# Where a planned instruction stream puts its counts, feature loads and pair steps

## The chip, the cores and the metric

One core of a Trainium2 chip runs the whole program. The metric is the device time of one execution in microseconds (us). The engines are TensorE (PE in the profile; PEld is its weight load), VectorE (DVE), ScalarE (ACT), GpSimd (POOL) and SyncE (SP, which here only issues DMAs). GpSimd issues DMAs too, from the same queue in which it computes.

## The reference

Four layers on one graph of 2708 nodes with 512 features; each adds its result to x and normalizes. Cut to what is computed:

```python
deg = maximum((adj != 0).sum(-1), 1)
# layer 0: weight a entry > 0 by itself plus 1/sqrt(number of such entries in its row)
inc = adj + mask / sqrt(sum(mask)) ;  x = layernorm(x + (inc @ x) / inc.sum(-1))
# layer 1: attention over the entries that are not 0, and a second branch
s = x @ W_sa @ a_l + (x @ W_sa @ a_r).T
e = where(adj != 0, exp(-leaky_relu(s)), 0)
x_a = (e / (e.sum(1) + 1e-5)) @ (x @ W_sa) ;  x_b = adj @ (x @ W_gcn) + b_gcn
x = layernorm(x + sigmoid(gate_a * x_a + gate_b * x_b))
# layer 2: powers of the adjacency
p = x ; o = x @ W[0] ;  for i in 1..3: p = adj @ p ; o += p @ W[i]
x = layernorm(x + o)
# layer 3: normalized adjacency with deg
x = layernorm(x + relu((d^-1/2 (adj + I) d^-1/2 @ x + x) @ W_out + b_out))
```

## The kernel before

All matrices are float32. Rows and columns are cut into two halves of 1354 nodes (h = 0 low, 1 high), and an adjacency product is done by a seven-product scheme for 2x2 blocks: products P1 to P7 of sums of the adjacency blocks (11, 12, 21, 22; the sums s1 to s4 are made in place by VectorE at line 419) with sums of the feature blocks (B11, B12, B21, B22; the sums T1 to T4, in lines 226 to 238). B12 is kept in the tile of T3. k counts tiles of 128 nodes, ten in each half and a rest.

There are seven sweeps over the adjacency. S[0] is layer 0; S[1] multiplies the plain adjacency (branch b of layer 1, and it writes the sums s1 to s4 to memory for later); S[2] multiplies the attention weights; S[3] to S[5] are the hops of layer 2; S[6] is layer 3. The first three go through four ranges of columns (384, 384, 256, 330 wide; S[0] begins with the 256), the others through two groups.

The order of the work is written by hand: `at(position, function)` puts a piece of work into a list, sorted by position. Sweep s starts at position 28 s, and a range takes 7 positions, one for each product; one position ("unit") of a 384-wide range is 40 matmul instructions on TensorE, of a 256- or 330-wide range likewise. So S[2] + 21.62 is in the fourth range of the third sweep. The framework then plans the instructions: each engine's queue is filled by list order among those that its own estimates hold ready, so an instruction may come earlier or later than in the list. Two things restrict this: all instructions of the first 3 times `strict` are tied to the one before them on their engine, and so are those of pieces put in with `hold` (True, or one engine). Such a tie (`add_manual_dep`, NoSync) only fixes the order in a queue [...]

Names and lines that the change and the prediction's steps touch:

- `next_x` (line 256): feature loads of S[1] from X1, which layer 0 writes range by range, issued on GpSimd (line 150 inside `move`); `x_sums` and `x_last` make T1 to T4.
- `layernorm` (line 598): bn_stats on VectorE, then the inverse root by a power on GpSimd (line 605), then VectorE or ScalarE scale (607, 610, 614).
- `extra1` (line 1031): `tally` counts the nonzero entries of each column of the first to fourth range in S[1] for `deg`: 44 VectorE instructions a range (lines 1039, 1042) into a mask tile, then `end` (six one-column matmuls, line 1056) and `rows`.
- `prep2` (line 1158): in S[2] the attention weights, two ScalarE instructions (1163, 1164) and one on VectorE (1165) for each tile.
- `pairs2` (line 1199): for two tiles of nodes at a time, one of each half, after a range of S[2]: b(0), b(1) multiply by W_sa (`seven`, line 692, accumulated by 701), c is the sigmoid, d and e the residual and layernorm, f the transposes (642), z the node sums (1193), g(0), g(1) the product with hop weights. There are 3 + 3 + 2 such pairs; the last range has no pairs.
- `sums2` (line 1139): sums of the weights for the pairs, partly in the memory of the mask tiles.
- `ext_loads`, `ext_sums` (lines 1331, 1340): added tiles; the hops multiply by [adjacency; transposed X2], and the sums of the X2 blocks are made here and stored (tensor Es, line 1345).
- `done6` (line 1639): end of layer 3 for one group and half.
- "ring" is a pool of 38 tiles for adjacency tiles, sums, ScalarE's e and the added tiles; an instruction that takes one waits until its last reader is done.

Of the kernel before, what the change touches and what calls it, by code (L numbers as in the profile page):

```python
# [28 lines left out]
KT = 11  # L29
# [17 lines left out]
KW = 2 * K2  # L47
# [21 lines left out]
def gnn_kernel(ctx: ExitStack, tc: tile.TileContext, x, adjT, w_sa, a_sa, w_gcn, b_gcn, wab, bab, w_hop, w_out,  # L69
# [106 lines left out]
    events = []  # L176

    held = set()

    def at(pos, fn, hold=False):  # L180

        def go():
            n = len(nc.cur_bb.bb.instructions)
            fn()
            for i in range(n, len(nc.cur_bb.bb.instructions)):
                if hold is True or nc.cur_bb.bb.instructions[i].engine == hold.engine:
                    held.add(i)

        events.append((pos, len(events), go if hold else fn))
# [60 lines left out]
    def x_load(src, k, s, eng):  # L250
        w = wt(k)
        q = x_source(src, k)[("B11", "B12", "B21", "B22").index(s)]
        t = b12_tile(k) if s == "B12" else new_x(s, k)
        move(eng, t[:w], q)

    def next_x(base, src, sums=0.95, halves=-0.25):


        q = nc.gpsimd

        ql = nc.scalar if base == S[1] else q
        at(base + 1.3, lambda: rest_x(src, ql))
        for k in range(KW):
            f = k / KT
            if (k * P) < RANGES[-1][0]:
                at(base - 5.8 + f, lambda k=k: x_load(src, k, "B11", q))
                at(base - 1.85 + f, lambda k=k: x_load(src, k, "B22", q))
                at(base - 1.84 + f, lambda k=k: x_load(src, k, "B12", q))
                at(base + (0.03 if base == S[1] else -1.15) + f, lambda k=k: x_sums(k), True)
                at(base - 0.85 + f, lambda k=k: x_load(src, k, "B21", q))  # L270
                at(base + 1.5 + f, lambda k=k: x_last(k), True)
            else:
                at(base + halves + 0.05 * (k - 8), lambda k=k: x_load(src, k, "B22", ql))
                at(base + max(halves, 0.1) + 0.05 * (k - 8), lambda k=k: x_load(src, k, "B21", ql))
                at(base + sums + 0.03 * (k - 8), lambda k=k: x_sums(k), True)
                at(base + 2.6 + 0.03 * (k - 8), lambda k=k: x_last(k), True)
# [321 lines left out]
    def layernorm(dsts, y, w, on_scalar=False, late=None):  # L598
        st = small.tile([P, 6], F32, name="st")
        nc.vector.bn_stats(st[:w], y[:w])  # L600
        mv = small.tile([P, 2], F32, name="mv")
        nc.vector.bn_aggr(mv[:w], st[:w])
        rstd = small.tile([P, 2], F32, name="rstd")
        nc.vector.tensor_scalar(rstd[:w, 0:1], mv[:w, 1:2], EPS, None, ALU.add)  # L604
        nc.gpsimd.tensor_tensor(rstd[:w, 1:2], rstd[:w, 0:1], neg_half[:w], ALU.pow)  # L605
        if on_scalar:
            nc.vector.scalar_tensor_tensor(rstd[:w, 0:1], mv[:w, 0:1], -1.0, rstd[:w, 1:2], ALU.mult, ALU.mult)
        for d, c0, c1 in dsts:
            if on_scalar:
                fn = lambda d=d, c0=c0, c1=c1: nc.scalar.activation(d[:w], y[:w, c0:c1], AF.Identity,  # L610
                                                                    bias=rstd[:w, 0:1], scale=rstd[:w, 1:2])
                fn() if late is None else late.append(fn)
                continue
            nc.vector.tensor_scalar(d[:w], y[:w, c0:c1], mv[:w, 0:1], rstd[:w, 1:2], ALU.subtract, ALU.mult)
# [125 lines left out]
    def tiles_of(R0, n):  # L740
        return list(range(R0 // P, (R0 + n + P - 1) // P))
# [287 lines left out]
    at(S[1] + 2.33 + 0.95 * (i - 1), scores_over)  # L1029

    def extra1(pb, r, R0, n, A):
        ts = tiles_of(R0, n)

        def tally(h, key, w=P):

            a = A[(r,) + key]
            if (R0, h) not in deg:
                deg[R0, h] = d = mask_tile()
                nc.vector.tensor_scalar(d[:w, :n], a[:w, :n], 0.0, None, ALU.not_equal)
            else:  # L1040
                d = deg[R0, h]
                nc.vector.scalar_tensor_tensor(d[:w, :n], a[:w, :n], 0.0, d[:w, :n], ALU.not_equal, ALU.add)  # L1042

        for ij, p in (("11", -0.6), ("21", 0.05), ("22", 1.05), ("12", 3.6)):
            for k in range(KW):
                at(pb + p + 0.8 * k / KT, lambda ij=ij, k=k: tally(int(ij[0]) - 1, (ij, k)), r == 0)
        for h, p in ((1, 2.0), (0, 4.5)):
            at(pb + p, lambda h=h: tally(h, ("r", h), KA))
            at(pb + p, lambda h=h: tally(h, ("r32", h), 32))

        def end(h):
            d = deg.pop((R0, h))
            ps = bank("ds", [P, 4])
            for i, q in enumerate(ts):
                wq = wt(q)
                nc.tensor.matmul(ps[:wq, i : i + 1], d[:, q * P - R0 : q * P - R0 + wq], ones_bf[:, 0:1], start=True,
                                 stop=True)
            for i, q in enumerate(ts):
                wq = wt(q)
                o = rdeg[:wq, h * KT + q : h * KT + q + 1]  # L1060
                nc.vector.tensor_scalar(o, ps[:wq, i : i + 1], 1.0, None, ALU.max)
                nc.vector.tensor_scalar(diag[:wq, h, q : q + 1], o, 1.0, None, ALU.add)
                nc.vector.reciprocal(o, o)

        def rows(h):
            to_rows(rdeg[:, h * KT + ts[0] : h * KT + ts[-1] + 1], len(ts),
                    DROW[h][0, ts[0] * P : (ts[-1] + 1) * P].rearrange("(k i) -> k i", i=P))

        at(pb + 2.6, lambda: end(1))
        at(pb + 3.7, lambda: rows(1))  # L1070
        at(pb + 5.2, lambda: end(0))
        at(pb + 6.3, lambda: rows(0))
# [78 lines left out]
            o, w = (W[2][2 * c + 1], w_sa) if k == 2 else (W[3][c][:, HD:], w_hop[3])  # L1151
            nc.scalar.dma_start(out=o, in_=w[c * P : (c + 1) * P, HD:])

    at(S[2] + 6.4, sums2)
    at(S[2] + 23.4, lambda: again(2))
    at(S[2] + 24.2, lambda: again(3))

# [9 lines left out]
    def extra2(pb, r, R0, n, A):  # L1167
        def rows(h):
            row[R0, h] = tmp("row")
            m = (n + P - 1) // P  # L1170
            src = SROW[R0, h][0:1, :]
            nc.sync.dma_start(out=row[R0, h][:, : m * P].rearrange("p (k i) -> p k i", i=P),
                              in_=bass.AP(tensor=src.tensor, offset=src.offset, ap=[[0, P], [P, m], [1, P]]))

        def share(o, s, t, w):
            nc.vector.tensor_scalar(o, s, 1e-5, None, ALU.add)
            nc.vector.reciprocal(o, o)
            nc.vector.tensor_tensor(o, o, gate[:w, t, 0:1], ALU.mult)

        at(pb - 1.6, lambda: rows(0))  # L1180
        at(pb - 1.0, lambda: rows(1))
        at(pb + 5.2, lambda: run_sums(R0, n, 0, share))
        at(pb + 4.7, lambda: run_sums(R0, n, 1, share))
# [15 lines left out]
    def pairs2(p0, R0, n, C, tiles):  # L1199
        Y = {}  # L1200
        at(p0 + 0.2, lambda: Y.update(row_sums({(i, c): C[1 - i, c] for i in range(2) for c in range(DC)}, n)))
        for i, (t0, lo, w) in enumerate(tiles):
# [6 lines left out]
            def b(part, ts=ts, lo=lo, w=w, xb=xb, H=H):  # L1209
                seven(part, Y, W[9], H, lo, w, xb, [rd[t][:w] for t in ts], xb)  # L1210
# [35 lines left out]
            at(p - 0.25, a)  # L1246
            at(p + 0.15, d)
            for j in range(2):
                at(p + 0.26 * j, lambda j=j, b=b: b(j))
                at(p + 0.45 + 0.02 * j, lambda j=j, e=e: e(j))  # L1250
                at(p + 0.84 + 0.06 * j, lambda j=j, f=f: f(j), nc.tensor)
                at(p + 1.22 + 0.22 * j, lambda j=j, g=g: g(j), nc.tensor)
            at(p + 0.4, c)
            at(p + 0.92, z)

    def done2(p0, dp, last, R0, n, h, C, tiles):
        if not last:
# [288 lines left out]


    for i in range(4):
        for g, p in enumerate((S[2] + 19.3 + 1.1 * i, S[3] + 6.6 + 1.3 * i)):
            a = ({}, g, i // 2, i % 2)  # L1550
            at(p, lambda a=a: ext_loads(*a))
            at(p + 0.5 + 0.6 * g, lambda a=a: ext_sums(*a))
# [53 lines left out]
        for r in (64, 96):  # L1606
            nc.gpsimd.dma_start(out=diag_r[r : r + 32, 2:3], in_=d2[KA - KR : KR, KT - 1 :])

    at(S[2] + 4.0, diag_ends)

    def finish_degrees():
        t = small.tile([24, P], F32, name="fd", bufs=1)
# [26 lines left out]
    def done6(p0, dp, g, i0, n, h, cc, tiles):  # L1639

        end = (g, h) == (1, 0)
        def finish(s, lo, w, x, y):

            nc.vector.scalar_tensor_tensor(x[:w], y[:w], 0.0, x[:w], ALU.max, ALU.add)
            layernorm([(x, 0, D)], x, w, True)
            r0 = i0 + s * n + lo
            move(nc.sync, out[h * NH + r0 : h * NH + r0 + w, :], x[:w])
# [77 lines left out]
    for n, i in enumerate(list(nc.cur_bb.bb.instructions)):  # L1725
        p = last if n < 3 * strict else done if n in held else {}
        if i.engine in p:
            tc.add_manual_dep(i, p[i.engine].name,
                              mybir.DependencyInfo(mybir.DependencyClass.NoSync, mybir.DependencyReason.DATA),
                              reason="order of the list")  # L1730
        if n < strict:
            last[i.engine] = i
        done[i.engine] = i


# [35 lines left out]
```

## Time and profile before

| | us |
|---|---|
| median of 3 runs | 2844.96 (2844.59 to 2845.8) |
| the profiled execution, its own time | 2845.44 |
| its span, first to last instruction | 2843.7 |
| TensorE busy | 2802.4 |
| VectorE busy | 2247.7 |
| GpSimd busy (DMA issue counted) | 617.2 |
| ScalarE busy | 533.7 |

Landmarks by the first matmul of product P1 in the timeline: fourth range of S[0] at 324.98, S[1] at 415.86, S[2] at 834.71, its second range at 945.39, third at 1084.96, fourth at 1193.69. The page gives busy shares and the costliest groups of instructions; the windows view gives busy time of each engine in stretches (length, PE, PEld, DVE, ACT, POOL, each with a count, then the granted TensorE clock, the DMA share and GB/s); the waits view has who waited for whom: us in total, times, longest; the timeline has start, length, engine, line, operation, out<-in, and in brackets the engine's idle time before it and what ended it. A float32 matmul appears as two matmul instructions.

### The profile page before, as it was taken

The numbers are of one execution on the slowest core, as the hardware profiler recorded it, in microseconds if no ns is written. First come the engines' busy times: TensorE is split into PE (matmuls) and PEld (weight loads), VectorE is DVE, ScalarE is ACT, GpSimd is POOL, SyncE is SP. The second block draws the span as 40 slices with busy tenths as digits, with TensorE's granted clock in tenths as the row PEclk, the third lists the DMA queues.
The fourth block names the chain that finished last, engine by engine and source line by source line (L and its number), as shares of the span: only waits on it lengthen the run. The fifth ranks groups of instructions, "written<-read, shape, count | busy, mean of one in ns | idle before, by whom it ended". The sixth has DMA issues, their size and how long they took to land.

```text
span 2843.7 us, 38764 instructions
## 1 busy us (share of the span) xinstructions
PE 2802.4 (99%) x11550; PEld 1939.7 (68%) x11550; DVE 2247.7 (79%) x5862; ACT 533.7 (19%) x1124; POOL 617.2 (22%) x1114
## 2 busy tenths in 40 slices
PE   7999999999999999999999999999999999999998
PEld 6899765658755667866666666666666666666665
DVE  6999699668737676775699778897888878899987
ACT  4644100101155353450100000000000100100001
POOL 0223223214310011223113033030330211601202
PEclk9999999999999999999999999999999999999999
DMA  8765476446534242665678667566675666854542
GB/s 234 241 195 184 140 228 218 150 131 196 189 92 139 78 152 69 203 194 158 205 205 255 192 208 234 163 210 203 197 235 173 189 194 180 243 167 146 179 142 90
DMA packets 370291, 511.72 MB, mean 180 GB/s; under 512 B 63632, under 2 KB 323460, under 8 KB 370080
## 3 DMA queue, kind: packets, MB, share of 16 engines
q1 hardware_dynamic: 303544, 371.61, 44.1%
q0 software_dynamic: 49376, 126.39, 13.3%
q10 hardware_dynamic: 17160, 11.24, 1.4%
q8 instruction: 92, 1.51, 0.2%
q14 instruction: 119, 0.97, 0.1%
HBM read 425.35 MB, written 83.66 MB: 179 GB/s over the span
## 4 chain that ended last, share of the span: by engine, by line
PE 86%; DVE 7%; issue 2%; DMA 1%; SPq 1%; ACT 1%; POOL 1%; POOLq 0%; DVEq 0%; ACTq 0%
PE accu L1437 12%; PE accd L1437 12%; PE accc L1437 12%; PE accu L489 7%; PE accd L489 7%; PE acca L1437 6%; PE ps L692 5%; PE accc L489 5%; PE acca L489 4%; PE accr L1508 2%; PE ps_d L653 2%; PE accd L475 2%; PE accc L475 2%; PE accu L475 2%; PE acca L475 1%
## 5 line engine op out<-in xcount | busy, mean ns | idle before, releaser
L1382 DVE TENSOR_TENSOR z<-z 128x339 f32<-128x339 f32 (+1 forms) x966 | 456.8, 507 | 10.9 <-PE accu L1437 2.9
L605 POOL TENSOR_TENSOR rstd<-rstd,neg_half 128x1 f32<-128x1 f32 (+3 forms) x91 | 61.2, 674 | 770.5 <-DVE rstd L604 484.0
L1455 ACT COPY q<-accu 128x338 f32<-128x338 f32 (+1 forms) x84 | 34.6, 443 | 996.5 <-PE accu L1437 836.2
L1437 PE MATMUL accc<-s,t 128*128 128x338 f32 (+1 forms) x644 | 198.1, 450 | 0.0
L1437 PE MATMUL accd<-z,t 128*128 128x338 f32 (+1 forms) x644 | 193.9, 448 | 1.4 <-DVE q L1519 1.4
L1437 PE MATMUL accc<-z,t 128*128 128x338 f32 (+1 forms) x644 | 193.5, 448 | 0.5 <-ACT q L1455 0.5
L1437 PE MATMUL accu<-z,t 128*128 128x338 f32 (+1 forms) x644 | 193.8, 448 | 0.0
L1570 POOL DMA_DIRECT2D Y<-y x192 | 104.8, 552 | 362.8 <-DVE y L1565 331.3
L419 DVE TENSOR_TENSOR a<-a,a 128x384 f32<-128x384 f32 (+2 forms) x330 | 164.2, 514 | 6.7 <-PE accu L489 5.5
L1437 PEld LDWEIGHTS accc<-s,t 128*128 128x128 f32 x644 | 120.9, 190 | 64.1 <-issue 7.5
L1437 PEld LDWEIGHTS accc<-z,t 128*128 128x128 f32 x644 | 122.0, 190 | 61.6 <-issue 1.0
L1437 PEld LDWEIGHTS accd<-z,t 128*128 128x128 f32 x644 | 121.9, 190 | 61.1 <-DVE q L1519 2.1
L1437 PEld LDWEIGHTS accu<-z,t 128*128 128x128 f32 x644 | 121.8, 190 | 59.9 <-issue 0.5
L1382 DVE TENSOR_TENSOR s<-z 128x338 f32<-128x338 f32 (+1 forms) x322 | 150.6, 506 | 9.1 <-PE accc L1437 7.7
L1461 DVE TENSOR_TENSOR q<-q,accd 128x338 f32<-128x338 f32 (+1 forms) x112 | 56.3, 503 | 122.4 <-PE accd L1437 122.4
L1163 ACT ACTIVATE e<-row,s_right 128x384 f32<-128x384 f32 (+5 forms) x176 | 95.7, 570 | 119.8 <-PE accc L489 28.5
L1165 DVE SCALAR_TENSOR_TENSOR a<-a,e 128x384 f32<-128x384 f32 (+2 forms) x160 | 77.0, 507 | 35.7 <-ACT e L1164 25.1
L1042 DVE SCALAR_TENSOR_TENSOR masks<-a,masks 128x384 bf16<-128x384 f32 (+2 forms) x152 | 76.0, 507 | 12.3 <-DMA a<-in_adjT 11.3
L422 POOL DMA_DIRECT2D As<-a x120 | 64.7, 542 | 88.3 <-DVE a L419 64.0
L829 DVE SCALAR_TENSOR_TENSOR s<-a,row 128x384 f32<-128x384 f32 (+2 forms) x152 | 75.8, 511 | 7.5 <-ACT row L814 7.5
L825 DVE TENSOR_TENSOR run<-run,a 128x384 f32<-128x384 f32 (+2 forms) x156 | 77.9, 499 | 1.4
L1164 ACT ACTIVATE e<-e 128x384 f32<-128x384 f32 (+5 forms) x176 | 78.7, 477 | 1.4
(787 smaller groups left out, 5957.6 us busy)
## 6 DMA issues: line engine op xcount, KB each, us to landing
z<-As SPq DMA_DIRECT2D x320, 169.5 KB
z<-As SPq DMA_DIRECT2D x320, 169.0 KB
a<-in_adjT SPq DMA_DIRECT2D x240, 192.0 KB
z<-in_adjT SPq DMA_DIRECT2D x240, 169.5 KB
z<-in_adjT SPq DMA_DIRECT2D x240, 169.0 KB
a<-in_adjT SPq DMA_DIRECT2D x120, 165.0 KB
a<-in_adjT SPq DMA_DIRECT2D x112, 128.0 KB
As<-a POOLq DMA_DIRECT2D x60, 192.0 KB, 3.5
```

What stands on the lines that cost most here:

```text
L419: nc.vector.tensor_tensor(A[r, dst, k][:, :n], A[r, a, k][:, :n], A[r, b, k][:, :n], op)
L475: nc.tensor.matmul(B[home, c][:, c0 : c0 + w], a[:, i * P : (i + 1) * P], x[:, d : d + w], start=bool(start and c0 == 0), stop=stop, skip_ ...
L489: nc.tensor.matmul(B[home, c][:, :n], X[STAT[p], k][:, c * P : (c + 1) * P], A[r, MOV[p], k][:, :n], start=bool(start and k == k0), stop=k ...
L692: nc.tensor.matmul(H[home][:w], Y[a, c][:, lo : lo + w], wop(v, c), start=part == 0 and home in "ud" and c == 0, stop=c == 1, skip_group_c ...
L825: nc.vector.tensor_tensor(run[R0, h][:w, :n], run[R0, h][:w, :n], t[:w, :n], ALU.add)
L1042: nc.vector.scalar_tensor_tensor(d[:w, :n], a[:w, :n], 0.0, d[:w, :n], ALU.not_equal, ALU.add)
L1163: nc.scalar.activation(e[:w, :n], row[R0, h][:w, :n], AF.Prelu, bias=s_right[:w, t : t + 1], alpha=0.01)
L1164: nc.scalar.activation(e[:w, :n], e[:w, :n], AF.Exp, scale=-1.0)
L1165: nc.vector.scalar_tensor_tensor(a[:w, :n], a[:w, :n], 0.0, e[:w, :n], ALU.not_equal, ALU.mult)
L1382: nc.vector.tensor_tensor(d[:, :n], Z[x + (k,)][:, :n], Z[y + (k,)][:, :n], op)
L1437: nc.tensor.matmul(B[home][:, :n], stat(v, k), a[:, :n], start=bool(start and k == 0), stop=k == nk - 1, skip_group_check=True)
L1570: nc.gpsimd.dma_start(out=rows[:, :, f * P : (f + 1) * P], in_=o[32 * f : 32 * (f + 1), : m * P].rearrange("p (b d) -> p b d", d=P))
```

## The change

Seven edits. The counts of the first range move from S[1] to S[2] (`tallies`, with positions of its own). The feature loads of B11, B22 and B12 for S[1] are tied behind the last layernorm power that stands before them in the list (`behind_power`, `powers`, `ties`); B11 of k > 2 stands half a unit later, and B21 at +0.45 in place of -0.85. Part b of the pairs is tied to its place on TensorE, and the steps of a pair stand a little further apart. The weight sums go from 6.4 to 6.8, `diag_ends` from 4.0 to 6.0. The added tiles of the first group are listed from S[2] + 18.6 on, 0.55 apart, in place of 19.3 and 1.1 apart. The first block of `done6` stands 0.35 later.

```diff
@@
     held = set()
+    powers, ties = [], []
@@
+    def behind_power(fn):
+        n = len(nc.cur_bb.bb.instructions)
+        fn()
+        if powers:
+            ties.extend((i, powers[-1]) for i in range(n, len(nc.cur_bb.bb.instructions)))
@@ next_x
-                at(base - 5.8 + f, lambda k=k: x_load(src, k, "B11", q))
-                at(base - 1.85 + f, lambda k=k: x_load(src, k, "B22", q))
-                at(base - 1.84 + f, lambda k=k: x_load(src, k, "B12", q))
+                for s, p in (("B11", 5.8 - 0.5 * (base == S[1] and k > 2)), ("B22", 1.85), ("B12", 1.84)):
+                    at(base - p + f, lambda k=k, s=s: behind_power(lambda: x_load(src, k, s, q)))
                 at(base + (0.03 if base == S[1] else -1.15) + f, lambda k=k: x_sums(k), True)
-                at(base - 0.85 + f, lambda k=k: x_load(src, k, "B21", q))
+                at(base + (0.45 if base == S[1] else -0.85) + f, lambda k=k: x_load(src, k, "B21", q))
@@ layernorm
         nc.gpsimd.tensor_tensor(rstd[:w, 1:2], rstd[:w, 0:1], neg_half[:w], ALU.pow)
+        powers.append(len(nc.cur_bb.bb.instructions) - 1)
@@ extra1
+        if r:
+            tallies(pb, r, R0, n, A, {"11": (-0.6, 0.8), "21": (0.05, 0.8), "22": (1.05, 0.8), "12": (3.6, 0.8)}, 2.0, 4.5)
+
+    def tallies(pb, r, R0, n, A, when, r1, r0):
...
-        for ij, p in (("11", -0.6), ("21", 0.05), ("22", 1.05), ("12", 3.6)):
+        for ij, (p, f) in when.items():
             for k in range(KW):
-                at(pb + p + 0.8 * k / KT, lambda ij=ij, k=k: tally(int(ij[0]) - 1, (ij, k)), r == 0)
-        for h, p in ((1, 2.0), (0, 4.5)):
+                at(pb + p + f * k / KT, lambda ij=ij, k=k: tally(int(ij[0]) - 1, (ij, k)))
+        for h, p in ((1, r1), (0, r0)):
@@
-    at(S[2] + 6.4, sums2)
+    at(S[2] + 6.8, sums2)
@@ extra2
+        if r == 0:
+            f = 1.0 * KT / KW
+            tallies(pb, r, R0, n, A, {"11": (-0.75, f), "21": (-0.15, f), "22": (1.0, 0.8 * f), "12": (3.45, f)}, 1.55, 3.95)
@@ pairs2
-                at(p + 0.26 * j, lambda j=j, b=b: b(j))
-                at(p + 0.45 + 0.02 * j, lambda j=j, e=e: e(j))
-                at(p + 0.84 + 0.06 * j, lambda j=j, f=f: f(j), nc.tensor)
-                at(p + 1.22 + 0.22 * j, lambda j=j, g=g: g(j), nc.tensor)
-            at(p + 0.4, c)
-            at(p + 0.92, z)
+                at(p + 0.3 * j, lambda j=j, b=b: b(j), nc.tensor)
+                at(p + 0.49 + 0.02 * j, lambda j=j, e=e: e(j))
+                at(p + 0.92 + 0.06 * j, lambda j=j, f=f: f(j), nc.tensor)
+                at(p + 1.38 + 0.22 * j, lambda j=j, g=g: g(j), nc.tensor)
+            at(p + 0.44, c)
+            at(p + 1.02, z)
@@
-        for g, p in enumerate((S[2] + 19.3 + 1.1 * i, S[3] + 6.6 + 1.3 * i)):
+        for g, p in enumerate((S[2] + 18.6 + 0.55 * i, S[3] + 6.6 + 1.3 * i)):
@@
-    at(S[2] + 4.0, diag_ends)
+    at(S[2] + 6.0, diag_ends)
@@ done6
+        if (g, h) == (0, 0):
+            p0 += 0.35
@@ at the end, after the ties of held pieces
+    instructions = list(nc.cur_bb.bb.instructions)
+    for i, j in ties:
+        tc.add_manual_dep(instructions[i], instructions[j].name, ..., reason="order of the list")
```

More of the change, by code (lines that the diff above doesn't have):

```diff
@@ L1733, in gnn_kernel @@
         done[i.engine] = i
+    instructions = list(nc.cur_bb.bb.instructions)
+    for i, j in ties:
+        tc.add_manual_dep(instructions[i], instructions[j].name,
+                          mybir.DependencyInfo(mybir.DependencyClass.NoSync, mybir.DependencyReason.DATA),
+                          reason="order of the list")
 def kernel(x, adj, L1_gnn_W_sa, L1_gnn_a_sa, L1_gnn_W_gcnb, L1_gnn_b_gcnb, L1_gnn_Wa, L1_gnn_ba, L1_gnn_Wb,
```

## The prediction

> **What bounds the kernel now.** I read, in this order, the page (busy shares), the windows view in 40 us steps (where TensorE is not full), the waits view for TensorE alone (which wait ends last), and the timeline around each gap.
>
> ```profile
> PE 2802.4 (99%) x11550; PEld 1939.7 (68%) x11550; DVE 2247.7 (79%) x5862; ACT 533.7 (19%) x1124; POOL 617.2 (22%) x1114
> ...
> 1200.00:1240.00 40.00, 36.12 (x139) 27.00 (x138) 26.58 (x66) 17.50 (x35) 9.85 (x17) 0.92 0.54 157
> ...
> PE ps L692 <- DVE d L1193: 4.4, 3, 3.4
> PE accd L489 <- DVE a L419: 3.3, 3, 1.5
> ...
> PE ps_t L642 <- DVE ld L614: 1.4, 3, 0.8
> PE accd L1437 <- DVE q L1519: 1.4, 1, 1.4
> ```
>
> TensorE is the bound: 99% busy, so a faster VectorE is worth nothing by itself and only TensorE's gaps can be won. In the 40 us windows it is short of 40 in the first 160 us (no edit reaches there), at 320 to 360, in scattered places of the third sweep (970 to 1260), at 2560 to 2640, and at the end. The window from 1200 is the only one in mid-run whose clock column (the third from the right) is not 1.00. The waits view names the releasers: VectorE each time.
>
> The first gap, in the timeline:
>
> ```profile
> 345.84 0.54 POOL L150 DMA_DIRECT2D B11B<-X  x1 [4.54 <-DMA X<-o]
> 346.39 0.56 POOL L605 TENSOR_TENSOR rstd<-rstd,neg_half 128x1 f32<-128x1 f32 x1
> ...
> 346.99 0.16 DVE L607 SCALAR_TENSOR_TENSOR rstd<-mv,rstd 128x1 f32<-128x1 f32 x1 [3.63 <-POOL rstd L605]
> ...
> 350.51 2.49 PE L489 MATMUL accd<-a,T1A 128*128 128x330 f32 x8 [1.10 <-DVE a L419]
> ...
> 356.70 3.58 PE L489 MATMUL accd<-a,T1C 128*128 128x330 f32 x11 [1.48 <-DVE a L419]
> ```
>
> GpSimd's queue holds a feature load (B11B) that waits for the store of X1 it reads; the layernorm's power stands behind it, VectorE behind the power (3.63 us), and the sums for accd come late: TensorE idles 0.69 + 1.10 + 1.48 = 3.27 us.
>
> The second gap:
>
> ```profile
> 1149.12 1.89 PE L692 MATMUL ps<-w,d 128*128 128x256 f32 x8
> ...
> 1228.89 0.57 ACT L1163 ACTIVATE e<-row,s_right 128x330 f32<-128x330 f32 x1 [4.09 <-DMA Es<-s]
> ...
> 1230.01 0.51 DVE L1165 SCALAR_TENSOR_TENSOR a<-a,e 128x330 f32<-128x330 f32 x1 [3.74 <-ACT e L1164]
> ...
> 1233.72 0.76 DVE L1193 TENSOR_TENSOR d<-xT 128x256 f32<-128x256 f32 x2
> ...
> 1234.20 3.78 PE L692 MATMUL ps<-w,d 128*128 128x256 f32 x8 [3.36 <-DVE d L1193]
> ```
>
> ScalarE waits 4.09 us for a ring slot that an added tile's store (Es) still reads; VectorE waits for ScalarE; the pair's node sums (L1193) are queued behind; TensorE idles 3.36 us. Then the same eight matmuls that took 1.89 us at 1149 take 3.78: the clock is halved.
>
> [...] the gaps up to 1.48 us leave the clock at 1.00, the 3.36 us gap is followed by half speed. [...] here the transfers on X land 2.3 to 6.7 us after issue, 3.6 in the median, and the trace's values are used.
>
> **The change part by part.**
>
> *Feature loads behind the last power (behind_power; B11 of k>2 half a unit later).* In the list the three layernorms of the third range's low half stand at S[0]+21.3 to 21.9, all B11 loads at 22.2 and after; it was the planner that put B11B ahead of the third power. The tie forbids it. The 3.63 us wait of VectorE goes, its sums come 3.63 us earlier, and the three gaps, 3.27 us together, fit in that. Gain 3.27; late next is nothing, since TensorE has no gap from 357 to 671. Bounds: 0 (another DMA in GpSimd's queue takes its place) to 3.27. The loads pay: B22 and B12 of k=3 to 7 now stand behind the powers of the next layernorms (run at 396.75 and 406.32), up to some 7 us later than B22C's 399.37; landing 3.6 us later gives 411, and the first product that reads T3C comes five steps of 1.29 us after 430.08, at 436.5. Hidden by some 20 us. B21 moves 1.3 units (12.9 us each: 40 matmuls of 0.323) later, to about 421.7 plus 3.6 us; T4A is first made at 444.86. Hidden by 19 us; they leave GpSimd's queue where powers stood (411.19), a gain off the path.
>
> *Counts out of the second sweep.* 44 VectorE instructions, 507 ns each by the L1042 row: 22.3 us leave 409 to 490, where VectorE was nearly full, but TensorE's windows there read 40.00 of 40.00. Gain 0.
>
> *Counts into the third sweep.* The same 44, with six tiny matmuls and two transposes that only change place. Cover:
>
> ```profile
> 840.00:860.00 20.00, 20.00 (x65) 9.95 (x65) 8.97 (x20) 18.09 (x29) 2.20 (x4) 1.00 0.38 123
> 860.00:880.00 20.00, 20.00 (x63) 11.78 (x62) 18.08 (x39) 14.74 (x30) 0.00 (x0) 1.00 0.63 185
> 880.00:893.00 13.00, 13.00 (x42) 7.68 (x41) 12.34 (x27) 8.93 (x18) 0.00 (x0) 1.00 0.52 142
> ```
>
> The figures are length, TensorE, its weight loads, then VectorE: 8.97, 18.08, 12.34. From 800 to 860 it works 15.36 + 8.97 of 60 us, so the 20 counts of "11" and "21" (10 us) fit. The ten of "22" and two of the rest fall in 860 to 893, which is full (30.4 of 33): at 0.47 us from start to start they push the sums back by 5.6 us. Those sums were made from 858.2 on and read by P5 from 872.28 on, 14 us of slack; the later ones (P6, from 885.18) have about as much. Cost 0; all 44 in that stretch would be 20.7 us, 6.7 more than the slack. The weight sums now wait for the mask's release (list S[2]+5.2, about 903), with the first pair's second product past 970 as their deadline. diag_ends is read only in the last sweep. Both 0.
>
> *Pairs' parts tied, steps spread.* Eight pairs. g moves from 1.22 to 1.38, f from 0.84 to 0.92, part b(1) from 0.26 to 0.30: between the transposes f and g now stand, in list order, both b parts of the next pair (28 matmuls, about 6 us), where b(1) came after g before. So the waits for L1193 (0.19 + 0.85 at 1125 and 1127) and for the accumulator at 1112.88 (0.20) go; that of the last pair's transpose (0.85 at 1256.71) is VectorE's crowding by added tiles, and goes with them. Gain 2.09. The transposes' own waits (0.47, 0.12, 0.26, 0.30, 0.21) stay: b(1) to f is six steps before and after.
>
> *Added tiles (ext) at S[2]+18.6 to 20.25 in place of 19.3 to 22.6.* 16 loads on SP, 16 VectorE sums, 16 stores on GpSimd (0.54 us each) leave the stretch after S[2]+21, where the 4.09 us wait arose, for the lull between the pairs of two ranges. Gain 3.36 idle plus the half clock: 3.78 - 1.89 for the ps eight, 3.65 - 2.38 for the accu eight after them, 3.16. SP's loads wait on X2T, stored by list 17.6, a unit (8.7 us here) ahead of the first; landing needs 3.6. If another ring wait takes its place, this gain is 0: lower bound; upper 6.52.
>
> *Last sweep, first group 0.35 units (3.5 us) later.* The row sums (eight of 0.42 us) stood between the rest additions (L1519) that free the banks accd waits for: 1.35 us. They go behind; gain 1.35. The 0.80 and 0.54 after it move with the block and I leave them: bounds 0 to 2.69.
>
> Sum of gains: 3.27 + 2.09 + 6.52 + 1.35 = 13.2. Against it I set new small waits of tied parts[...]; I take 1.4, what the five waits of the already tied f parts add up to. Net 11.8: span 2843.7 becomes 2831.9; the profiled execution has 1.74 around its span and stands 0.48 above the median of the runs, so 2833.2.
>
> **Rivals.**
> (a) Forecast: 2833, own range 2828 to 2838. Chance 0.60.
> (b) A ring or node-sum wait of over 3.4 us stays near S[2]+23 and keeps its half clock: 13.2 - 6.5 = 6.7 gained, 2838.3, with 2 us either way. For: ScalarE, ring and VectorE stay crowded there by the fourth range. Against: the tile it waited for is gone from there. 0.20.
> (c) The ties don't do what they say, since the planner's choices fall out alike and other stalls take the place: 2844, within 1 us. Against: B11B ahead of a power is now forbidden outright. 0.06.
> (d) Slower: tied parts b stand at the head of TensorE's in-order queue when their row sums (L682) or VectorE's reading of the accumulators come late. A stand of 3.4 us costs 6.5 with the clock; two are paid by the gains, from three of the 16 parts on it is slower: 19.5 - 13.2 gives 2851. For: the planner works by estimates, and VectorE is fuller in this sweep. Against: before, part b started on its list place at 1201.46 with no wait. 0.14.
>
> **How the numbers follow.** A measurement can tell about 0.2% (5.7 us: below 2839.3 is faster). (a) is wholly faster; of (b) 0.14 is faster and 0.06 the same; (c) is the same; (d) slower. Faster 0.74, same 0.12, slower 0.14. The range from 2827 (all upper bounds) to 2843 takes in (b) and leaves out (d).
>
> **What would show it.** After: no B11 load before the third power near 342, no TensorE gap at 347 to 357; no wait of ScalarE on Es near 1229 and clock 1.00 in all windows from 40 to 2800; no count in the second sweep's first range and 44 before 930 with TensorE full there; the accd wait near 2573 gone. Wrong if a gap of over 3.4 us appears anywhere in the third sweep, or if TensorE waits for L419 or for the tied L692 parts by more than 3 us in sum.

## The result and the profile after

The changed kernel takes 2861.31 us (median of 4 runs, 2857.52 to 2863.15) against 2845.16 for the kernel before (4 runs beside it, 2844.59 to 2845.8): ratio 1.0055, 95% interval 1.0038 to 1.0072. It is slower, outside the range. The profiled execution took 2857.52, its span 2855.6; it is the fastest of the four, so what is read from it below accounts for 11.9 us of span, not for the whole difference of 16 us between the medians.

Line numbers have shifted: L419, L564, L614 and L692 of before are L426, L571, L622 and L700 here, and some experiments shift them a few lines further. The waits of TensorE:

```profile
PE ps_n L644 <- DVE P1c L571: 13.4, 1, 13.4
...
PE ps L700 <- DVE d L690: 5.2, 2, 4.0
...
PE accd L496 <- DVE a L426: 1.4, 1, 1.4
```

The first line has no counterpart before: one wait of 13.4 us, longer than all gaps the prediction worked with. To see which stages gained and lost, I took the first matmul of P1 in each stage from the timelines and subtracted neighbours (us; e5 and e8 are experiments below; "rest" is the rest product at 1430.61 before, "last sweep" begins with the one at 2558.21):

| stage | before | after | e5 | e8 |
|---|---|---|---|---|
| fourth range of S[0], to S[1] | 90.88 | 88.48 | 88.07 | 88.95 |
| first range of S[1] | 101.10 | 116.32 | 101.55 | 101.09 |
| rest of S[1], to S[2] | 317.75 | 317.94 | 317.94 | 318.18 |
| S[2], to the rest product | 595.90 | 596.71 | 596.85 | 594.57 |
| last sweep, to the end of the span | 285.49 | 283.88 | 284.20 | 283.92 |

One stage holds the whole loss of this execution: 15.2 us in the first range of S[1], from which the counts were taken. The windows view of it (length, PE, PEld, DVE, ACT, POOL, then the clock):

```profile
412.00:416.00 4.00, 3.89 (x13) 2.09 (x11) 3.88 (x9) 0.00 (x0) 3.17 (x6) 1.00 0.43 102
416.00:429.00 13.00, 0.00 (x0) 0.00 (x0) 0.73 (x2) 0.00 (x0) 5.00 (x10) 0.65 0.79 255
429.00:434.00 5.00, 4.71 (x14) 3.03 (x15) 5.00 (x12) 0.00 (x0) 2.36 (x5) 0.55 0.72 257
```

For 13 us TensorE does nothing and VectorE 0.73 us of work; then five us run at a clock of 0.55. So VectorE is not busy, it waits. For what, the timeline says:

```profile
414.40 1.48 DVE L426 TENSOR_TENSOR s<-a,a 128x384 f32<-128x384 f32 x3
415.20 0.32 ACTq L150 DMA_DIRECT2D B11R<-X  x1
...
417.30 0.59 SPq L310 DMA_DIRECT2D r<-in_adjT  x1
...
418.00 3.75 SPq L417 DMA_DIRECT2D a<-in_adjT  x3
...
428.27 0.56 DVE L426 TENSOR_TENSOR a<-a,a 128x384 f32<-128x384 f32 x1 [12.38 <-DMA a<-in_adjT]
...
428.74 0.90 DVE L571 TENSOR_TENSOR P1c<-P1c,acca 128x330 f32<-128x330 f32 x2
...
429.29 0.88 PE L644 MATMUL ps_n<-ident,P1c 128*128 128x128 f32 x2 [13.41 <-DVE P1c L571]
```

At the head of VectorE's queue stands a sum at L426 (s1, block 21 plus block 22). It waits 12.38 us for an adjacency tile whose load SP issued at 418.00. Behind it stand the last additions of the first sweep (L571), which TensorE needs for its transposes. The queue went in order here: VectorE ran nothing from 415.88 to 428.27, and the additions started at 428.74, next after the sum. Before, the same additions ran at 417.20, and VectorE went on with the counts and the layernorms:

```profile
417.20 0.90 DVE L564 TENSOR_TENSOR P1c<-P1c,acca 128x330 f32<-128x330 f32 x2
...
419.62 0.56 DVE L1042 SCALAR_TENSOR_TENSOR masks<-a,masks 128x384 bf16<-128x384 f32 x1
420.09 0.56 DVE L419 TENSOR_TENSOR a<-a,a 128x384 f32<-128x384 f32 x1
...
421.56 0.56 DVE L419 TENSOR_TENSOR a<-a,a 128x384 f32<-128x384 f32 x1
...
438.77 0.55 DVE L1042 SCALAR_TENSOR_TENSOR masks<-a,masks 128x384 bf16<-128x384 f32 x1
439.24 0.56 DVE L419 TENSOR_TENSOR a<-a,a 128x384 f32<-128x384 f32 x1
```

After the additions (L564) these are the counts (L1042) and the in-place sums of the kernel before: two s1 sums at 420 and 421, and none from there to 439, while the counts and the first sweep's layernorms go through. That gives **theory O**. An s1 sum overwrites the 21 tile, so it must come after the count that reads that tile; that count was a held piece, tied behind the instruction that stood before it in the list, where the pieces of the first sweep's end stand as well. By this theory the held counts thus kept the s1 sums behind that end. With the counts gone the planner was free to put a sum ahead, where its load is not there yet. **Rivals**: the feature loads, moved later, crowd the transfers (L); the counts cost time in the third sweep (C).

The third sweep, predicted to gain 7.2 us, lost 0.8. Its timeline after:

```profile
1198.48 0.51 DVE L1359 TENSOR_TENSOR s<-a,a 128x338 f32<-128x338 f32 x1 [4.23 <-DMA a<-X2T]
...
1201.45 1.60 DVE L1359 TENSOR_TENSOR a<-a,a 128x338 f32<-128x338 f32 x3 [2.46 <-DMA a<-X2T]
...
1203.76 17.45 SPq L417 DMA_DIRECT2D a<-in_adjT  x18
...
1209.23 0.57 ACT L1175 ACTIVATE e<-row,s_right 128x330 f32<-128x330 f32 x1 [3.87 <-DMA Es<-a]
1209.63 0.50 DVE L1177 SCALAR_TENSOR_TENSOR a<-a,e 128x330 f32<-128x330 f32 x1 [2.74 <-DMA a<-in_adjT]
...
1218.74 0.50 DVE L1177 SCALAR_TENSOR_TENSOR a<-a,e 128x330 f32<-128x330 f32 x1 [2.12 <-DMA a<-in_adjT]
...
1219.57 0.42 DVE L690 TENSOR_TENSOR d<-C,P1c 128x256 f32<-128x256 f32 x1
...
1220.04 1.22 PE L700 MATMUL ps<-T1D,d 128*128 128x256 f32 x2 [4.01 <-DVE d L690]
```

ScalarE's wait for Es is still there, 3.87 us in place of 4.09, only earlier: 2.8 us after the fourth range's first matmul (1206.46), where it was 35.2 after it (1193.69). The kernel before ran the added tiles' loads in four groups from 1163 to 1239; now they all fall between 1179 and 1204, right where the fourth range fetches its adjacency tiles (18 of them queue on SP from 1203.76). Their sums head VectorE's queue twice with nothing loaded (4.23 and 2.46 us). The attention weights then wait for their own adjacency tiles (2.74 and 2.12 us), and the row sums (L690) of the first pair, which stand behind the last of these waits, come late: TensorE idles 4.01 and 1.19 us, and the clock is at half for 6.83 us from 1218.56.

### The profile page after: what moved, and what is told of

The parts are those of the page before. It is cut to its first block, busy times and chain, and to the rows that moved or that the text cites. A ratio compares the mean times of both kernels' runs of the same rounds, so it can differ in the third digit from the quotient of the medians.

```text
span 2855.6 us, 38750 instructions
## 1 busy us (share of the span) xinstructions
PE 2802.5 (98%) x11550; PEld 1939.2 (68%) x11550; DVE 2246.1 (79%) x5862; ACT 531.1 (19%) x1122; POOL 616.4 (22%) x1114
## 3 DMA queue, kind: packets, MB, share of 16 engines
q8 instruction: 92, 1.51, 0.2%
## 4 chain that ended last, share of the span: by engine, by line
PE 85%; DVE 6%; DMA 4%; issue 2%; POOL 1%; SPq 1%; ACT 1%; POOLq 0%; ACTq 0%; DVEq 0%
PE accd L1452 12%; PE accc L1452 12%; PE accu L1452 12%; PE accu L496 6%; PE accd L496 6%; PE accc L496 6%; PE acca L1452 6%; PE ps L700 5%; PE acca L496 3%; PE accr L1523 3%; PE ps_d L661 2%; PE accd L482 2%; PE accc L482 2%; PE accu L482 1%; DMA a<-in_adjT 1%
## 5 line engine op out<-in xcount | busy, mean ns | idle before, releaser
L426 DVE TENSOR_TENSOR a<-a,a 128x384 f32<-128x384 f32 (+2 forms) x330 | 163.3, 509 | 17.9 <-DMA a<-in_adjT 12.8
```

Of the source, the lines that this page charges most:

```text
L426: nc.vector.tensor_tensor(A[r, dst, k][:, :n], A[r, a, k][:, :n], A[r, b, k][:, :n], op)
```

## The experiments

Every kernel was timed beside the kernel before on the same chip; the chips differ by up to 3.6 us, so the ratios are compared.

**e1, e2, e3: take an edit back.** e1 puts the counts back into S[1], held; e2 puts the feature loads back (untied, old positions); e3 does both.

```diff
+ at(pb + p + f * k / KT, lambda ...: tally(...), r == 0)      # e1, e3; for every range in extra1, none in extra2; f is 0.8
+ at(base - 5.8 + f, lambda k=k: x_load(src, k, "B11", q))     # e2, e3; B22, B12, B21 alike
```

> The changed kernel with the first range's counts back in the second sweep, tied as before; all else changed. Theory O (order): without the counts the planner puts the s1 sums of S[1], which wait for adjacency loads that land late, ahead of the P1c additions that TensorE's transposes (ps_n) need. Then the 13.4 us gap near 416 is gone (under 1 us) and so is its half clock: 2861.3 - 15.5 = 2846, within 2. Theory L (loads): the later, bunched feature loads fill the queues and delay the adjacency loads; the gap stays over 8 us: 2856 to 2863.

> The changed kernel with the feature loads of S[1] listed and tied as before; counts stay in the third sweep. Theory O: the s1 sums stay ahead of the P1c additions, the gap near 416 stays over 8 us, and the wait of 3.3 us near 350 comes back: 2856 to 2865. Theory L: the gap is gone: 2846 to 2849.

> Counts and feature loads both as before; pairs, added tiles, sums2, diag_ends and the last sweep as changed. Both theories: no gap near 416, the 3.3 us near 350 are back. What is left is the worth of the other edits: if the third sweep gains nothing and the last one 1.6, 2843.5 within 1.5; by the prediction's sum (9 in the third sweep, 1.4 in the last) 2835.

| | time, us | ratio to before (95%) | TensorE gaps between 412 and 442, us |
|---|---|---|---|
| after | 2861.31 | 1.0055 (1.0038 to 1.0072) | 13.41 |
| e1 | 2849.01 | 1.0006 (0.9999 to 1.0013) | 2.05 |
| e2 | 2861.98 | 1.0054 (1.0039 to 1.0069) | 0.90, 7.05, 1.65 |
| e3 | 2848.47 | 1.0005 (0.9996 to 1.0013) | none |

With the counts back the loss goes; with the feature loads back it stays. In e2 the first additions get through, and the wait stands one step on:

```profile
431.44 1.06 DVE L427 TENSOR_TENSOR a<-a,a 128x384 f32<-128x384 f32 x2 [9.34 <-DMA a<-in_adjT]
...
436.57 2.93 PE L497 MATMUL accu<-a,B11D 128*128 128x384 f32 x4 [7.05 <-DVE B11D L623]
```

An s1 sum waits 9.34 us for its adjacency tile, and TensorE waits 7.05 us for the layernorm's B11D behind it, with the feature loads as before. Rival L falls. In e3 the first gap is back too (0.88, 1.10, 1.48), and the edits that are left bring nothing: the last sweep is 1.5 us shorter than before, the third 3.1 longer.

e1 came only in part as expected: 2.05 us of the gap stay, and nothing is won against the kernel before.

```profile
401.14 0.43 DVE L231 TENSOR_TENSOR T1B<-T3B,B11B 128x256 f32<-128x256 f32 x1 [1.33 <-DMA T3B<-X]
...
417.51 0.90 DVE L571 TENSOR_TENSOR P1c<-P1c,acca 128x330 f32<-128x330 f32 x2
...
418.06 0.73 PE L644 MATMUL ps_n<-ident,P1c 128*128 128x128 f32 x2 [2.05 <-DVE P1c L571]
```

TensorE reaches S[1] 2.6 us earlier than in the kernel before (413.27 for 415.86), but the additions run no earlier (417.51 for 417.20), and the first range of S[1] takes 104.00 us. In e3, the same kernel with the old feature loads, it takes 101.10. VectorE's waits from 380 to 418 sum to 6.9 us in e1 and 3.7 in e3; two of those in e1 are for loads of B12 (kept in T3B). In e8 below, which ties the B11 loads alone, the additions run at 412.76 and the range takes 101.09. So with the counts held in S[1], the other steps of the feature-load edit (B22 and B12 tied, B11 and B21 later) cost what the B11 ties had gained.

**e4: guard the additions alone.** The s1, s2 and s4 sums of the first range are tied on VectorE behind the P1c additions.

```diff
+ if nm == "P1c" and base == S[0]: guards.append(len(nc.cur_bb.bb.instructions) - 1)
+ if base == S[1] and r == 0 and dst != "s3":
+     ties.append((len(nc.cur_bb.bb.instructions) - 1, guards[-1]))
```

> The changed kernel with one thing more: the s1, s2 and s4 sums of the first range of S[1] are tied behind the P1c additions of the last range of S[0] on VectorE (order only). Counts stay in the third sweep, loads stay tied. Theory O: the gap near 416 falls from 13.4 to under 3 us: 2845 to 2850. Theory L: the loads land as late as they did and TensorE waits for something else of the same length within 20 us: 2856 to 2863.

It missed: 2859.91, ratio 1.0049 (1.0034 to 1.0064), as rival L had it. Its timeline:

```profile
416.42 0.74 PE L648 MATMUL ps_n<-ident,P1c 128*128 128x128 f32 x2 [0.48 <-DVE P1c L573]
429.05 1.72 DVE L426 TENSOR_TENSOR a<-a,a 128x384 f32<-128x384 f32 x3 [10.80 <-DMA a<-in_adjT]
435.48 2.29 PE L498 MATMUL accu<-a,B11D 128*128 128x384 f32 x3 [9.48 <-DVE B11D L626]
```

The guarded additions are on time (0.48), but the sum that waits (10.80) now stands ahead of the layernorm that makes B11D, and TensorE waits 9.48 us there. Theory O reads this as a guard that ends too early; e4 alone does not tell it from rival L, but e2 and the next run do.

**e5: guard the whole end of the first sweep.** As e4, but behind the layernorm of the last tiles.

```diff
  layernorm(o, y, w, not last, None if last else got.setdefault("late", []))
+ if last and not h: guards.append(len(nc.cur_bb.bb.instructions) - 1)
```

> The changed kernel, with the s1, s2 and s4 sums of the second sweep's first range tied on VectorE behind the last layernorm of the first sweep (the counts stay in the third sweep). Theory O (the moved counts had held those sums back; without them a sum that waits for its adjacency tile heads VectorE's in-order queue): the 13.4 us gap near 416 and the 9.5 us gap near 426 are both gone, no more than 2 us of TensorE idle between 412 and 450, time 2846 to 2850, that is 11 to 15 us under the changed kernel's 2861. Rival L (the adjacency loads land late in this kernel and whatever reads them stalls): the gap moves on to product P2 near 437 with 5 us or more and the time stays at 2855 or above. Rival C (the 44 counts cost time in the third sweep): the gap goes, but the time stays 3 us or more above that of the kernel with the counts put back (2849.0).

2841.01 us, ratio 0.9992 (0.9985 to 0.9999): 0.6% below the changed kernel's ratio, by an order on one queue, with the counts where the change put them. Its windows:

```profile
412.00:442.00 30.00, 29.44 (x99) 17.41 (x98) 26.61 (x74) 1.82 (x4) 20.16 (x38) 1.00 0.87 282
```

TensorE is short by 0.56 of 30 us, 0.48 of them a wait for the additions. The stage table shows the range at 101.55 in place of 116.32. The time lies under the 2846 to 2850 that I expected, which came from e1's chip, where the kernel before takes 3.6 us longer. Rival C falls as it was put: S[2] takes 596.85 us here with the counts in it, 601.80 in e1's profile without them.

**e6, e7, e12: the third sweep's edits, on e5.** e6 lists the added tiles as before, e7 the pairs as before, e12 both.

```diff
- S[2] + 18.6 + 0.55 * i
+ S[2] + 19.3 + 1.1 * i                                # e6, e12
- at(p + 0.3 * j, lambda j=j, b=b: b(j), nc.tensor)
+ at(p + 0.26 * j, lambda j=j, b=b: b(j))              # e7, e12; other steps alike
```

> The kernel of e5 with the added tiles of the first group back on their old places (19.3 and 1.1 apart). Theory E (listed earlier, their sums head VectorE's queue waiting for their loads and make the tied pair parts stand for the row sums): the TensorE waits for the row sums and accumulators between 1195 and 1225 fall under 1 us in sum, but the stall near 1230 of the kernel before comes back with its half clock; net within 2 us of e5. Rival P (the spread and tied pair steps make those waits): the waits between 1195 and 1225 stay within 1 us of those of e5.

> The kernel of e5 with the pairs' steps and part b as before (not tied, old distances), added tiles in their new places. Theory E: waits of TensorE between 1195 and 1225 remain, over 3 us in sum, perhaps under other names. Rival P: TensorE has no wait for the row sums over 0.5 us there, the half clock near 1218 goes, and the time is 4 to 7 us under e5.

> The kernel of e5 with both the pairs' parts and the added tiles as before: of the change it keeps the counts' move, the feature loads and the last sweep's step. If the third sweep's edits bring nothing in either direction, ratio to the kernel before 0.9983 to 0.9995, as e5, e6, e7; if the two undid each other's gain or loss, it lies 3 us or more off e5.

| | ratio to before (95%) | S[2], us | TensorE's waits of 0.9 us and more in the fourth range |
|---|---|---|---|
| e5 | 0.9992 (0.9985 to 0.9999) | 596.85 | 2.23, 1.09, 1.72 at 1194 to 1204 |
| e6 | 0.9990 (0.9983 to 0.9996) | 597.58 | 2.04 at 1233 |
| e7 | 0.9991 (0.9984 to 0.9998) | 594.59 | 1.30, 3.10 at 1202 and 1207 |
| e12 | 0.9996 (0.9989 to 1.0003) | 598.65 | 5.30 at 1230 |

The lines of e7 between 1195 and 1225, where part b of the pairs is not tied:

```profile
1203.12 0.70 PE L702 MATMUL ps<-T2D,d 128*128 128x256 f32 x2 [1.30 <-DVE d L692]
1210.00 0.70 PE L702 MATMUL ps<-T3B,W 128*128 128x256 f32 x2 [3.10 <-DVE ld L711]
```

The row-sum waits do not need the tie: they stay in e7 (1.30 us, and 3.10 us for an accumulator that VectorE reads late), and they go in e6, where the added tiles are back. So it is the added tiles' place that makes them. But where the tiles leave, a wait near 1230 returns. In e6 it is 2.04 us for a sum and 0.81 for the node sums; in e12 it is the node sums alone:

```profile
1235.52 3.78 PE L702 MATMUL ps<-w,d 128*128 128x256 f32 x8 [5.30 <-DVE d L1212]
```

Each arrangement has its stall of 2 to 5 us in the same 40 us, and the four times can't be told apart with certainty.

**e8: the kernel before with two edits alone**, the B11 ties and the last sweep's step.

```diff
- at(base - 5.8 + f, lambda k=k: x_load(src, k, "B11", q))
+ at(base - 5.8 + f, lambda k=k: behind_power(lambda: x_load(src, k, "B11", q)))
@@ done6
+ if (g, h) == (0, 0): p0 += 0.35
```

> The kernel before with two of the edits alone: the B11 feature loads tied behind the last layernorm power, and the first block of the last sweep 0.35 later. By the prediction's terms: 3.27 and 1.35 us gained, 2840.5 to 2841.5, ratio 0.9984. Rival (the time won at the first gap is lost again at the next stall, since what ends there is VectorE or a transfer): only the 1.35 stays, 2843.5 to 2844.

2839.66, ratio 0.9987 (0.9980 to 0.9993), about 3.5 us under the kernel before beside it. It is the lowest ratio of all, though its interval overlaps those of e5, e6, e7 and e12, and it beats both kernels. At the first gap one wait remains, 1.51 us of the 3.27; the last sweep gains 1.57 (285.49 to 283.92).

**e9: the counts' move alone, in the kernel before.**

```diff
- at(pb + p + 0.8 * k / KT, lambda ...: tally(...), r == 0)
+ tallies(...)     # in extra2 for r == 0, positions of the change; sums2 6.8, diag_ends 6.0
```

> The kernel before with the counts' move alone (and the later places of the weight sums and diag_ends that go with it). Theory O: this alone makes the loss. An s1 sum stands ahead of the P1c additions, TensorE idles 8 to 14 us between 412 and 440 and has the clock halved after it, ratio to the kernel before 1.003 to 1.006. Rival: the gap needs the feature loads' ties as well; ratio within 0.9985 to 1.001.

2861.96, ratio 1.0053 (1.0038 to 1.0068). From its timeline:

```profile
418.71 0.56 DVE L419 TENSOR_TENSOR a<-a,a 128x384 f32<-128x384 f32 x1 [4.79 <-DMA a<-in_adjT]
...
430.04 1.05 DVE L419 TENSOR_TENSOR a<-a,a 128x384 f32<-128x384 f32 x2 [7.35 <-DMA a<-in_adjT]
435.15 2.57 PE L489 MATMUL accu<-a,B11D 128*128 128x384 f32 x4 [3.64 <-DVE B11D L614]
```

The move alone makes the loss: two sums head the queue (4.79 and 7.35 us), and TensorE's four gaps there sum to 7.6 us, a little under the expected 8; the clock from 412 to 442 averages 0.84, and the range takes 114.79 us for 101.10.

**e10: the counts stay in S[1], but not held.** One word less than the kernel before:

```diff
- at(pb + p + 0.8 * k / KT, lambda ...: tally(...), r == 0)
+ at(pb + p + 0.8 * k / KT, lambda ...: tally(...))
```

> The kernel before with its counts left in the second sweep but no longer held (not tied to their neighbours on the engines). Theory H (what protected the first sweep's end was the hold, not the work itself): s1 sums and counts of the 22 tiles are then planned ahead of the last layernorms, and TensorE idles 4 us or more between 412 and 440, ratio above 1.001. Rival F (the counts merely filled VectorE's time): no gap over 2 us there, ratio within 0.0015 of 1.

2859.63, ratio 1.0048 (1.0033 to 1.0063):

```profile
430.62 0.56 DVE L1042 SCALAR_TENSOR_TENSOR masks<-a,masks 128x384 bf16<-128x384 f32 x1 [8.47 <-DMA a<-in_adjT]
436.31 2.93 PE L489 MATMUL accu<-a,B11D 128*128 128x384 f32 x4 [4.73 <-DVE B11D L614]
```

The work is in the same sweep, and the loss is there: now a count itself heads the queue and waits 8.47 us. TensorE's gaps between 412 and 442 are 3.17, 4.73 and 0.34 us. What protected the end of the first sweep was the hold.

**e11: the rest loads on GpSimd's queue**, in the changed kernel, to see whether the adjacency load is late because SP's queue stands on ScalarE's rest loads.

```diff
- at(base + 1.3, lambda: rest_x(src, ql))
+ at(base + 1.3, lambda: rest_x(src, q))
```

> The changed kernel, with the rest tiles of the features of the second sweep loaded on GpSimd's queue in place of ScalarE's. Theory S [...]: SP gets past the r32 load 2 us or more before 417.3, the s1 sum at the head of VectorE's queue waits under 9 us in place of 12.4, the gap near 416 shrinks by 3 us or more, time 2852 to 2858. Rival M (the loads are late because the ring tiles they need come free late or the DMA engines are full then): the wait stays at 11 us or more and the time within 2 us of the changed kernel.

2857.09, ratio 1.0035 (1.0022 to 1.0048):

```profile
414.24 0.58 SPq L310 DMA_DIRECT2D r<-in_adjT  x1
414.93 1.38 SPq L417 DMA_DIRECT2D a<-in_adjT  x3
...
421.43 0.56 DVE L426 TENSOR_TENSOR a<-a,a 128x384 f32<-128x384 f32 x1 [4.19 <-DMA a<-in_adjT]
```

SP passes the r32 load 3 us earlier (414.24 for 417.30), the sum waits 4.19 in place of 12.38, and TensorE 5.46 in place of 13.41. The waits view of the changed kernel agrees: it puts 4.1 us of SP's wait before the r32 load down to ScalarE's load of B11R. So SP's queue stood on ScalarE's rest loads here, and that made part of the stall's length, not the stall: with the wrong order 5.46 us remain.

## Why the prediction was wrong, point by point

**Counts out of the second sweep, "Gain 0": the step that failed.** I summed the work that leaves (22.3 us of VectorE) and found TensorE full there. I did not ask what those instructions had been ordering, though the diff shows their hold going with them and "The kernel before" says what a hold is. The range lost 15.2 us: 13.41 of idle TensorE, and about 2 for the 4.2 us that it then ran at half clock. e9 (the move alone, 1.0053), e10 (the hold taken off, 1.0048) and e5 (another guard, 0.9992) show it. Nor is the work that leaves worth nothing once the order is kept: with the feature loads as changed, the range takes 101.55 us in e5 and 104.00 in e1, where the counts stand before the additions. No rival of the prediction had it: (d) looked for the loss in the third sweep. With 101.1 us for this range the span would have been 2840.4. But the other terms did not come either: with the order repaired e5 gains 2.1 us of the forecast 11.8.

**Counts into the third sweep, "Cost 0": right where they run, open further on.** TensorE reads 90.00 of 90.00 from 840 to 930 in the changed kernel. The first range of S[2] is 0.55 us longer in every kernel that carries them (111.23 for 110.68); the six small matmuls and two transposes that came along are the likely reason. e5 and e7 carry the counts and are no slower than before. With the pairs and added tiles of before, though, S[2] takes 598.65 and 599.94 us with the counts (e12, e9) and 594.57 to 597.34 without (before, e8, e10), and the stall near 1230 is longer (5.30 and 5.69 us for 3.36 to 4.13). These are single profiles, so a cost of some 3 us there is not excluded.

**Feature loads, 3.27: right in mechanism, too large.** No B11 load stands before the third power (342.24) any more and two of the three waits are gone; 1.41 us remain. The prediction had "late next is nothing"; VectorE is late next: from 344.77 to 357 its timeline shows no idle time at all, and the sum that TensorE waits for (353.43) simply has its turn late. The stage gained 2.40. "Hidden by some 20 us" was wrong for the loads that pay: it asked when TensorE reads T3C, but VectorE needs the B12 tiles from 401 on for its own sums, in the order of its queue, and in e1 it waits for two of them. How much of the 2.9 us that e1 loses there (104.00 for 101.10 in e3) is theirs stays open.

**Pairs and added tiles, 2.09 + 6.52 - 1.4: wrong.** Both named falsifiers came: a gap over 3.4 us (4.01 at 1216.03) with half clock, and 5.2 us of waits of the tied L692 parts in sum. Their cause was rival (d)'s place, the row sums, but not its mechanism: the tie isn't needed (e7). What failed is the sentence that the added tiles go to a "lull": I took the list's positions for the time of execution. Before, the planner already ran three of the four groups between 1163 and 1196, and packed closer they meet the fourth range's loads and ring slots. The stage got 0.8 us longer, and in e5, e6, e7 and e12 it lies within 3 us of before.

The pairs' own waits did go, but others came in their place. The three of 0.20, 0.19 and 0.85 us that the prediction named between 1112 and 1128 are absent from the changed kernel; these are new or longer:

```profile
987.61 0.66 PE L650 MATMUL ps_t<-ident,ld 128*128 128x128 f32 x4 [0.77 <-DVE ld L622]
...
1073.79 0.83 PE L846 MATMUL rs<-ones_f,run 128*128 128x1 f32 x6 [0.70 <-DVE run L833]
...
1173.36 1.09 PE L650 MATMUL ps_t<-ident,ld 128*128 128x128 f32 x8 [0.73 <-DVE y L707]
```

Over the second and third ranges the waits of TensorE that the timeline shows sum to 2.48 us before and 2.44 after, so of the 2.09 nothing was won there.

**Last sweep, 1.35: right.** The accd wait near 2573 is gone and the stage is 1.61 shorter. The wait of 0.80 that I left standing became 0.33.

**The clock: too few readings.** (b) and (d) charge half clock to stands of 3.4 us, from two readings: none after gaps up to 1.48 us, half after 3.36. In the runs a gap of 3.10 us came without half clock (e7) and one of 1.55 us with it (e6); see the last section.

**The range's lower end, 2827 "all upper bounds": a wrong sum.** The upper bounds 3.27, 2.09, 6.52 and 2.69 make 14.6 us, which gives 2830.

## What to carry to other kernels

Before moving an instruction out of a stage, ask what it orders as well as what it costs: a held instruction that reads a tile keeps every later writer of that tile behind it, and the writer, once free, can be planned to the head of its queue before its load has landed: here VectorE stood 12.38 us behind one such sum, and TensorE 13.41. If such an order is needed, state it by itself and up to the last instruction on the path (e5), since a guard that ends early only moves the wait (e4). And read where a piece runs from the trace, not from its place in a list that a planner reorders.

## What the runs showed of the hardware

**Half clock came here in multiples of 3.41 us, and the length of one gap did not decide it.** Between 30 and 2830 us the clock is at half once before (6.83 us from 1233.50) and twice after (13.65 us from 419.84, 6.83 from 1218.56); the two of after begin 798.72 us apart, 234 times 3.413. Of the 3.41 us just ahead of each of the three, TensorE idled 2.67, 3.41 and 2.53 us, still at clock 1.00; in each stretch the clock column reads 0.50. In the experiments the time of like matmuls shows the clock. After e7's gap of 3.10 us, two ps matmuls take 0.59 us from 1210.53 on, as they did ahead of it (1204.09): no half clock. In e6, after a gap of 1.55 us, ten accd matmuls take 3.67 us at 1172.56; in e5, after one of 0.94 us, the same ten take 2.40. In e9, after gaps of 1.34 and 0.60 us that end at 419.73 and 420.66, two transposes take 0.63 us at 422.76, and 0.38 at 420.82.

**SP's queue stood 4.1 us on a load of ScalarE's.** In e11, moving ScalarE's rest loads to GpSimd's queue let SP's queue go on 3 us earlier (414.24 for 417.30), with no data between the two. The waits view names the load that SP waited for (B11R, 4.1 us); why it had to was not shown.
